# Layer 0's stores of two steps sent in one run, ahead of the keys' transfers of the same step

## The chip, the cores and the metric

The kernel runs on one NeuronCore of a Trainium2 chip. The time is that of the device for one execution, in microseconds (us). Before the change three runs took 5833.54, 5835.1 and 5843.29 us; their median is 5835.1. The engines are TensorE (PE in the profile, PEld for its weight loads), VectorE (DVE), ScalarE (ACT), GpSimd (POOL) and SyncE (SP). SP computes nothing here: it issues the DMA transfers, one after the other in the order of the program.

## The reference, cut to what matters

A picture of 4 x 16 x 512 x 512 fp32 values goes through four layers. The change is in layer 0, a block with windowed attention; the three others are stacks of convolutions and are only named here.

```python
def _L0_conv_ref(x, ...):                       # C = 16, HEADS = 2, WS = 8, HID = 64
    pos = conv_general_dilated(x, pos_w, 3x3, feature_group_count=Cc)
    x = x + pos + pos_b
    xt = transpose(x.reshape(B, Cc, H * W), (0, 2, 1))
    y = _aff(xt, alpha1, beta1, color1)         # y @ color.T * alpha + beta
    win = y cut into windows of 8 x 8           # 4 * 64 * 64 windows of 64 tokens
    q, k, v = win @ qkv_w.T + qkv_b             # q scaled by hd ** -0.5
    attn = softmax(einsum('bhnd,bhmd->bhnm', q, k))
    out = einsum('bhnm,bhmd->bhnd', attn, v) @ proj_w.T + proj_b
    x = xt + out put back in place
    h1 = gelu(_aff(x, alpha2, beta2, color2) @ fc1_w.T + fc1_b)
    return x + (h1 @ fc2_w.T + fc2_b)

x = _L0_conv_ref(x, ...)
x = _L1_conv_ref(x, ...)    # quantised 3x3 convolution, batch norm over the picture, clip
x = _L2_conv_ref(x, ...)    # two 3x3 convolutions with a residual
x = _L3_conv_ref(x, ...)    # 3x3 convolution, then a pointwise layer of 128
```

Layer 1 quantises by the largest absolute value of its whole input. So layer 0 has to end before layer 1 can round its first value. The kernel therefore keeps the maximum of each piece of layer 0's result in a tile `peak`.

## The kernel before, in words

**Steps.** `window_attention` is layer 0. It cuts the picture into 64 steps. A step works on 64 columns of all strips, which gives 128 partitions of four row groups (`U` = `V` = 4) and 8 windows each. Each step has two halves. The first is the attention: a loop over k from 1 to 7 with a piece before it and one behind it, so eight pieces in all. Piece k turns eight key tiles (`values`, a transpose on TensorE, L338), multiplies keys by queries (`scores`, L353), takes the exponential on ScalarE (L361), multiplies by the values (`attend`, L374), and divides (`divide`: two transposes L389 and a reciprocal L394 on VectorE, a multiplication L396 on GpSimd). The second half is the projection, the two layers of the MLP (L421 with Gelu at L426), and, mixed with them, the depthwise convolution (L287) and the queries (L319) of the steps that follow. ScalarE loads its table for the exponential at the end of a step (L574) and the one for Gelu between the halves (L540). So the time from a load at L574 to the next at L540 is that of the first half, and from L540 to L574 that of the second.

**The order.** Layer 0 runs in an order written out by hand (`manual_schedule`) for all five queues: each engine takes its instructions as the Python code emits them. A DMA waits on SP until what it reads is written and what it overwrites is read. SP's later transfers stay behind it.

**The keys.** `y2` holds the keys of all windows of a step in the form that `scores` and `values` need. There is one such buffer, in four quarters. When a quarter has been read by pieces 2q and 2q + 1 of step n, `turn_keys` (L310) fills it with the keys of step n + 1: 8 transfers of 32 KB, 32 in a step. They are called behind the division at k = 1, 3, 5 and 7.

**The outputs.** `output` (fc2 on TensorE, L432, and the sum with the residual on VectorE, L437) is called at the head of the step behind its own, between the first scores and the loop over k. It writes `xo`, one buffer that takes the results of two steps, an even one and the odd one behind it. When the odd step's part is there, `store` puts 32 stores of 64 KB into a Python list, with 8 largest values to be taken. The results of the steps n - 2 and n - 1 are therefore complete at the head of step n, where n is even. `send` takes stores from the list and issues them at L90 on SP; each writes 16 partitions of `xo` to the picture `x1` in the chip's memory. The next `output`, at the head of the odd step n + 1, writes `xo` again; it has to wait until the stores have read it.

**Banks.** `output` uses the four PSUM banks 5, 4, 6 and 7. `values(1)`, at k = 1, writes bank 6 and has to wait until the sum at L437 has read it.

**The load.** At the end of a step SP issues the load of the picture's part for the step four ahead (L185, 1320 KB into one of two buffers `x`). It waits until the depthwise convolution has read the buffer. The data are used two steps later.

The lines around the change are these:

Of the kernel before, what the change touches and what calls it, by code (L numbers as in the profile page):

```python
# [86 lines left out]
def _store_block(nc, x1, src, b, r0, cols, queues=None):  # L87

    rows = x1.rearrange("m (r c) b x -> (m r) c b x", r=2)[r0 + 1 : r0 + 1 + WS, :, b, cols]
    (next(queues) if queues else nc.sync).dma_start(rows.rearrange("m c x -> c m x"), src)  # L90
# [53 lines left out]
def window_attention(ctx: ExitStack, tc, xw, x1, hots, m, v, peak):  # L144
# [15 lines left out]
    U = V = 4  # L160
# [122 lines left out]
    def depthwise(n, tap, u):  # L283

        dy, dx = divmod(tap, 3)
        for vv in range(V):
            nc.tensor.matmul(  # L287
                bank(u)[quad(vv)], taps[quad(u), tap, :],
                xts[n][quad(u), vv, dy : dy + WS, dx : dx + BW],
                start=tap == 0, stop=tap == 8,  # L290
            )

    def position(n):

        y = px.tile([P, U, N], F32, tag="y", name=f"y{n}", bufs=3)
        for u in range(U):
            if u // 2:
                nc.scalar.activation(  # L298
                    by_window(y[:, u]), by_row(bank(u)), AF.Identity, bias=v("pos_b")
                )  # L300
            else:
                nc.vector.tensor_scalar(  # L302
                    by_window(y[:, u]), by_row(bank(u)), v("pos_b"), None, ALU.add
                )
        return y

    def turn_keys(y, vv):
        for u in range(U):
            for w in range(2):
                nc.sync.dma_start(  # L310
                    y2[32 * u + C * w : 32 * u + C * w + C, vv, :, w, :],
                    y[32 * vv + C * w : 32 * vv + C * w + C, u, :].rearrange(
                        "p (j t) -> p j t", t=T
                    ),
                )

    def query(y, h, vv, b, scalar=False):
        for u in range(U):
            nc.tensor.matmul(  # L319
                b[quad(u)], wg[h][quad(vv)], y[quad(vv), u, :], start=True, stop=True  # L320
            )
        out, src = g[:, vv, :, h, :], b.rearrange("p (j t) -> p j t", t=T)
        if scalar:
            nc.scalar.activation(out, src, AF.Identity, bias=gb[:, h : h + 1])
        else:
            nc.vector.tensor_scalar(out, src, gb[:, h : h + 1], None, ALU.add)
# [6 lines left out]
    def values(k):  # L333

        vv, jl = k // 2, 4 * (k % 2)
        b, t = bank(4 + 2 * (k % 2)), yts[k % 3]
        for jj in range(4):
            nc.tensor.transpose(  # L338
                b[:, P * jj : P * jj + P],
                y2[:, vv, jl + jj].rearrange("p w t -> p (w t)"), m("ident"),  # L340
            )
        src = b.rearrange("p (a w c) -> p a w c", w=2, c=C)
        if 0 < k < 7:
            nc.scalar.copy(t[:, :, 0:3:2], src)
        else:
            nc.vector.tensor_copy(t[:, :, 0:3:2], src)  # L346

    def scores(k, n):

        vv, jl = k // 2, 4 * (k % 2)  # L350
        for i, jj in ((0, 0), (0, 1), (1, 0), (0, 2), (1, 1), (0, 3), (1, 2), (1, 3)):
            for u in (2 * i, 2 * i + 1):
                nc.tensor.matmul(  # L353
                    bank(u)[:, P * jj : P * jj + P],
                    y2[quad(u), vv, jl + jj].rearrange("p w t -> p (w t)"),
                    g[quad(u), vv, jl + jj].rearrange("p h t -> p (h t)"),
                    start=True, stop=True,
                )
        e = px.tile([P, U, 4, P], F32, tag="e", name=f"e{n}_{k}", bufs=3)
        for i in range(2):  # L360
            nc.scalar.activation(  # L361
                e[:, 2 * i : 2 * i + 2].rearrange("p u j t -> p u (j t)"),
                pairs[i], AF.Exp,
            )
        return e

    def attend(e, k):

        t = yts[k % 3]
        for jj in range(4):  # L370
            for u in range(U):
                for w in range(2):
                    half = slice(64 * w, 64 * w + 64)
                    nc.tensor.matmul(  # L374
                        bank(4 + 2 * (k % 2) + w)[quad(u), P * jj : P * jj + P],
                        t[half, U * jj + u, w : w + 2].rearrange("p d c -> p (d c)"),
                        e[half, u, jj, :],
                        start=True, stop=True,
                    )

    def part(t, k):
        vv, jl = k // 2, 4 * (k % 2)
        return t[:, vv, jl : jl + 4].rearrange("p j h t -> p (j h t)")
# [18 lines left out]
    def turn_back(t, k):  # L402
        nc.vector.transpose(part(o, k), t.rearrange("p b w c -> p (b w c)"))
# [25 lines left out]
    def output(y, xo, hids, us, banks, n):  # L429

        for k, (vv, hd) in enumerate(hids):
            nc.tensor.matmul(  # L432
                bank(banks[k // 4])[quad(vv)], m("fc2"), hd, start=True, stop=True
            )
        at = BW * (n % 2)
        for u, i in zip(us, banks):
            nc.vector.tensor_tensor(  # L437
                xo[:, u, :, at : at + BW].rearrange("p a (j x) -> p a j x", x=WS),
                by_window(bank(i)), by_window(y[:, u]), ALU.add,
            )  # L440
        if n % 2:
            store(xo, n // 2, us)
# [22 lines left out]
    def send(k, queues=None):  # L465
        for _ in range(min(k, len(stores))):
            src, u, r, cb = stores.pop(0)
            _store_block(nc, x1, src, u, r, slice(XW * cb, XW * cb + XW), queues)
# [40 lines left out]
    for n in range(STEPS):  # L509
        more, ahead = n + 1 < STEPS, n + 2 < STEPS  # L510
        taken, asked = [0] * U, [0] * V

        def block(what, i, b, scalar=False):
            at = i % 4
            if what == "q" and more:
                query(ys[n + 1], asked[at], at, b, scalar)
                asked[at] += 1
            elif what == "d" and ahead:
                depthwise(n + 2, taken[at], at)
                taken[at] += 1  # L520
                if taken == [9] * U:
                    ys[n + 2] = position(n + 2)

        values(0)
        es, ts = {0: scores(0, n)}, {}
        if last:

            output(*last)
        for k in range(1, 8):
            es[k] = scores(k, n)  # L530
            values(k)
            attend(es[k - 1], k - 1)
            ts[k - 1] = divide(k - 1, n, nc.gpsimd)
            if 1 < k < 7:
                turn_back(ts[k - 2], k - 2)
            if k % 2 and more:
                turn_keys(ys[n + 1], k // 2)
            highest_output()
            send(5)
        nc.scalar.preload_act_table_set("gelu_and_others")  # L540
        attend(es[7], 7)
        ts[7] = divide(7, n, nc.gpsimd)
        for k in (5, 6, 7):
            turn_back(ts[k], k)
        free = iter((4, 5, 6, 7, 4, 5))
        for i, what in enumerate("qqddddqqqqdddddd"):
            block(what, i, bank(next(free)) if what == "q" else None, True)
        if more:
            highest(n + 1)
        highest_output()  # L550
        y = ys.pop(n)
        project(y)
        if n % 2 == 0:
            xo = px.tile([P, U, WS, XW], F32, tag="xo", name=f"xo{n}", bufs=1)
        if not more:
            flag = bounded()

        hids, units = [], itertools.cycle((6, 7, 4, 5))  # L560
        for i, what in enumerate("ddddhdhddhqhddhqhddhdhddhdhddhdhddhdhddddhdh"):
            if what == "h":
                q = len(hids)
                hids.append(hidden(y, q // 4, i % 4, bank(next(units)), n))
                if not more and q in (5, 9, 13):
                    u = q // 4 - 1
                    output(y, xo, hids[q - 5 : q - 1], (u,), (u,), n)
                    send(8, queues)
            else:
                block(what, i, bank(next(units)) if what == "q" else None)  # L570
        if n + 4 < STEPS:
            xts[n + 4] = load(n + 4)
        if more:
            nc.scalar.preload_act_table_set("natural_log_exp_and_others")  # L574
        last = (y, xo, hids, range(U), (5, 4, 6, 7), n)
# [795 lines left out]
```

## Time and profile before

| | |
|---|---|
| median of three runs | 5835.1 us |
| profiled execution | 5832.97 us |
| its span | 5831.2 us |
| mean granted TensorE clock | 0.987 |
| TensorE busy | 5512.4 us |
| ScalarE busy | 3464.1 us |
| VectorE busy | 3723.4 us |

The span is the time from the first to the last instruction that the profile records; the time of the execution is 1.8 us longer. Layer 0 reaches to about 3250 us of the span; layers 1 to 3 follow. The page's second part cuts the span into 40 slices of 145.8 us. Its digits are busy shares in tenths; layer 0 has slices 1 to 22.

The transfers of layer 0, from the page's sixth part, are:

```
x<-in_xw_dram SPq DMA_DIRECT2D x64, 1320.0 KB
y<-y SPq DMA_DIRECT2D x2048, 32.0 KB
x<-xo SPq DMA_DIRECT2D x1008, 64.0 KB
```

The first are the loads, the second the keys, the third the stores; 16 more stores of the last step go through GpSimd's queue. From 169 to 3190 us of the span, a store keeps SP for 303 ns at least, 435 in the median and 2017 at most; a key transfer for 585, 598 and 2139 ns. This is the time of the issue, not of the transfer.

In a line of the timeline the numbers are the start in us from the span's start, the time taken in us, the engine (SPq is SP's DMA queue), the line of the kernel, the operation, what is written and read, and how many instructions were merged. In brackets stands how long the engine was idle before and what ended this.

### The profile page before, as it was taken

To read this page: it belongs to the slowest core of one execution; us is meant where nothing else is said; L and a number is where in the kernel's file an instruction comes from. 1 tells how busy PE (TensorE), PEld (TensorE's weight loads), DVE (VectorE), ACT (ScalarE), POOL (GpSimd) and SP (SyncE) were. 2 spreads that over 40 slices of the span, in tenths; PEclk is the share of its full clock that TensorE was granted. 3 is DMA by queue.
4 is the path that set the end of the run, shared out by engine and by line. 5 is a ranking of instruction groups with operands and counts; after the bars stand their busy time and mean duration, and the time that the engine had idled before them with its cause. 6 is when DMAs were issued, how large, how long until landed. Compare 5 with 4: busy or idle time off the path is not lost. (4 is left out here: it accounts for less than half of the span.)

```text
span 5831.2 us, 268523 instructions
## 1 busy us (share of the span) xinstructions
PE 5512.4 (95%) x120912; PEld 3058.4 (52%) x120912; DVE 3723.4 (64%) x5806; ACT 3464.1 (59%) x4739; POOL 707.4 (12%) x692
## 2 busy tenths in 40 slices
PE   7999999999999999999999676999999999999999
PEld 5666666666666666666666333333333333333333
DVE  4666666666666666666666564666666666666666
ACT  4777777777777777777776453444444444444444
POOL 1111111111111111111111451000000000000000
PEclk9999999999999999999999898999999999999999
DMA  2232323233333333332332796666666666666663
GB/s 78 69 77 68 81 67 72 69 79 70 78 72 75 75 72 77 71 79 69 79 70 47 170 252 169 168 169 171 165 171 167 169 171 166 170 167 170 171 165 103
DMA packets 626194, 677.47 MB, mean 116 GB/s; under 512 B 355856, under 2 KB 485008, under 8 KB 616848
## 3 DMA queue, kind: packets, MB, share of 16 engines
q1 hardware_dynamic: 624240, 658.76, 47.3%
q8 instruction: 953, 15.61, 1.1%
q14 instruction: 201, 1.65, 0.1%
q0 software_dynamic: 512, 1.05, 0.1%
q10 hardware_dynamic: 288, 0.39, 0.0%
HBM read 222.45 MB, written 134.48 MB: 61 GB/s over the span
## 5 line engine op out<-in xcount | busy, mean ns | idle before, releaser
L361 ACT ACTIVATE e<-pair 128x1024 f32<-128x1024 f32 x1024 | 992.9, 1022 | 436.7 <-PE pair L353 436.0
L287 PE MATMUL pair<-x,taps 32*32 32x512 f32 x18432 | 1082.2, 600 | 2.2 <-DVE y L302 1.2
L1205 ACT ACTIVATE hid<-tb,vec 128x512 f32<-128x512 f32 x1024 | 620.0, 688 | 518.1 <-PE tb L1197 518.0
L389 DVE STREAM_TRANSPOSE a<-bank 128x512 f32<-128x512 f32 x1024 | 669.8, 692 | 346.5 <-PE bank L374 313.3
L396 POOL TENSOR_TENSOR t<-a,r 128x512 f32<-128x512 f32 x512 | 542.0, 1059 | 2662.2 <-DVE r L394 2598.5
L426 ACT ACTIVATE hid<-bank,f1b 128x512 f32<-128x512 f32 x1024 | 648.3, 687 | 345.2 <-PE bank L421 281.6
L353 PE MATMUL pair<-g,y 32*128 32x128 f32 x16384 | 762.8, 288 | 29.5 <-ACT y L298 25.8
L353 PEld LDWEIGHTS pair<-g,y 32*128 32x128 f32 x16384 | 650.4, 187 | 189.6 <-issue 77.4
L421 PE MATMUL bank<-y,fc_e 32*32 32x512 f32 x8192 | 738.3, 606 | 1.0 <-DVE y L414 1.0
L1207 DVE TENSOR_SCALAR hid<-tb,vec 128x512 f32<-128x512 f32 x1024 | 695.7, 742 | 2.7 <-PE tb L1197 2.6
L1197 PE MATMUL tb<-ye,mat 32*128 32x512 f32 x4096 | 637.7, 624 | 0.3 <-DVE hid L1207 0.3
L374 PE MATMUL bank<-e,yt 64*32 64x128 f32 x32768 | 610.0, 276 | 28.3 <-DVE yt L346 21.4
L287 PEld LDWEIGHTS pair<-x,taps 32*32 32x32 f32 x18432 | 495.4, 103 | 171.2 <-issue 66.3
L374 PEld LDWEIGHTS bank<-e,yt 64*32 64x32 f32 x32768 | 465.6, 106 | 127.3 <-issue 99.1
L1217 PE MATMUL tb<-hid,mat 128*32 128x512 f32 x4096 | 466.0, 595 | 41.6 <-DVE hid L1207 41.6
L1197 PEld LDWEIGHTS tb<-ye,mat 32*128 32x128 f32 x4096 | 267.0, 183 | 323.4 <-issue 219.9
L1122 PE MATMUL tb<-zo,cw 64*32 64x512 f32 x3096 | 362.8, 594 | 14.8 <-issue 8.9
L338 PE MATMUL bank<-mat,y 128*128 128x128 f32 x2048 | 338.9, 288 | 36.1 <-DVE xo L437 36.0
L1122 PE MATMUL tb<-xo,cw 64*32 64x512 f32 x3096 | 365.0, 599 | 8.4 <-issue 6.6
L1122 PE MATMUL tb<-xe,cw 64*32 64x512 f32 x3072 | 360.3, 599 | 0.0
L1122 PE MATMUL tb<-ho,cw 64*32 64x512 f32 x3072 | 355.2, 591 | 3.1 <-issue 3.1
L1122 PE MATMUL tb<-ze,cw 64*32 64x512 f32 x3072 | 356.8, 594 | 0.0
(180 smaller groups left out, 7051.7 us busy)
## 6 DMA issues: line engine op xcount, KB each, us to landing
x<-in_xw_dram SPq DMA_DIRECT2D x64, 1320.0 KB
zo<-ze SPq DMA_DIRECT2D x512, 128.5 KB
ho<-he SPq DMA_DIRECT2D x512, 128.5 KB
xo<-xe SPq DMA_DIRECT2D x512, 128.5 KB
y<-y SPq DMA_DIRECT2D x2048, 32.0 KB
tx<-x SPq DMA_DIRECT2D x256, 256.0 KB
out_dram<-xe SPq DMA_DIRECT2D x128, 512.0 KB
x<-xo SPq DMA_DIRECT2D x1008, 64.0 KB
```

The source lines that it names most:

```text
L287: nc.tensor.matmul(bank(u)[quad(vv)], taps[quad(u), tap, :], xts[n][quad(u), vv, dy : dy + WS, dx : dx + BW], start=tap == 0, stop=tap == 8,)
L353: nc.tensor.matmul(bank(u)[:, P * jj : P * jj + P], y2[quad(u), vv, jl + jj].rearrange("p w t -> p (w t)"), g[quad(u), vv, jl + jj].rearra ...
L361: nc.scalar.activation(e[:, 2 * i : 2 * i + 2].rearrange("p u j t -> p u (j t)"), pairs[i], AF.Exp,)
L374: nc.tensor.matmul(bank(4 + 2 * (k % 2) + w)[quad(u), P * jj : P * jj + P], t[half, U * jj + u, w : w + 2].rearrange("p d c -> p (d c)"), ...
L389: nc.vector.transpose(a[:, 512 * w : 512 * w + 512], bank(4 + 2 * (k % 2) + w))
L396: engine.tensor_tensor(t.rearrange("p b w c -> p w b c"), top, r.unsqueeze(3).to_broadcast([P, 2, 16, C]), ALU.mult,)
L421: nc.tensor.matmul(b[quad(k)], fc1[quad(vv), quad(k)], y[quad(vv), u, :], start=True, stop=True,)
L426: nc.scalar.activation(hd, b, AF.Gelu, bias=f1b)
L1122: nc.tensor.matmul(p[r][_quad(2 * f + w)], weights[_half(r), odd, dx, :], src[_half(r), f, dx : dx + W], start=dx == 0, stop=dx == 2,)
L1197: nc.tensor.matmul(p[q], w1[_quad(q), 1 - par, :], inner(src)[_quad(q), f, :], start=True, stop=True,)
L1205: nc.scalar.activation(hd, p[q], AF.Relu, bias=v("l3_b1"))
L1207: nc.vector.tensor_scalar(hd, p[q], v("l3_b1"), 0.0, ALU.add, ALU.max)
```

## The change

At k = 1, behind the first division and ahead of the first `turn_keys`, `send(8 * U)` issues up to 32 stores. The `send(5)` at the end of each of the seven passes is gone. `store` fills the list for each even step alone, so the call finds 32 stores in the even steps 2 to 62 and none in the odd ones. The stores of the last two steps are sent by other calls, which stay as they are.

```diff
             ts[k - 1] = divide(k - 1, n, nc.gpsimd)
             if 1 < k < 7:
                 turn_back(ts[k - 2], k - 2)
+            if k == 1:
+                send(8 * U)
             if k % 2 and more:
                 turn_keys(ys[n + 1], k // 2)
             highest_output()
-            send(5)
         nc.scalar.preload_act_table_set("gelu_and_others")
         attend(es[7], 7)
```

## The prediction

> **What bounds the kernel now.** I read the page first (shares, the 40 slices), then the waits of the first stage by total, then two neighbouring steps in the timeline, then the DMA share microsecond by microsecond.
>
> ```profile
> PE 5512.4 (95%) x120912; PEld 3058.4 (52%) x120912; DVE 3723.4 (64%) x5806; ACT 3464.1 (59%) x4739; POOL 707.4 (12%) x692
> ...
> PE   7999999999999999999999676999999999999999
> ...
> DMA  2232323233333333332332796666666666666663
> ```
>
> TensorE is the bound from slice 2 to the end, and the change touches only layer 0, slices 1 to 22. There the 16 DMA engines are busy 20 to 30% of the time: a mean that hides bursts. What counts is each piece of idle time on PE. The waits of 200 to 3100 us, PE's own first, then DVE's on xo and the two largest of SP's queue (these three for 200 to 3000):
>
> ```profile
> PE bank L338 <- DVE xo L437: 36.0, 24, 3.1
> PE pair L353 <- ACT y L298: 24.5, 59, 0.4
> PE bank L374 <- DVE yt L346: 19.4, 32, 0.8
> ...
> DVE xo L437 <- DMA x<-xo: 103.2, 19, 7.1
> ...
> SPq L185 <- PE bank L421: 404.7, 28, 15.5
> SPq L310 <- PE bank L338: 360.8, 71, 7.9
> ```
>
> The columns are total us, times, longest. PE's largest wait is 36.0 us in 24 pieces, for xo, and xo waits in turn for the stores of the xo before it. All 24 pieces are in odd steps. Step 19 (odd, its outputs at 1022 us) beside step 18 (even, at 970 us), DVE, then PE, then SP:
>
> ```profile
> 967.53 0.69 DVE L346 COPY yt<-bank 128x512 f32<-128x512 f32 x1
> 970.87 1.50 DVE L437 TENSOR_TENSOR xo<-bank,y 128x512 f32<-128x512 f32 x2 [2.65 <-PE bank L432]
> ...
> 1016.75 0.69 DVE L346 COPY yt<-bank 128x512 f32<-128x512 f32 x1
> 1022.93 2.48 DVE L437 TENSOR_TENSOR xo<-bank,y 128x512 f32<-128x512 f32 x4 [5.49 <-PE bank L432]
> ...
> 974.46 0.66 PE L338 MATMUL bank<-mat,y 128*128 128x128 f32 x4
> ...
> 1024.87 0.66 PE L338 MATMUL bank<-mat,y 128*128 128x128 f32 x4 [1.15 <-DVE xo L437]
> ...
> 1012.43 5.72 SPq L310 DMA_DIRECT2D y<-y  x8
> 1018.20 2.11 SPq L90 DMA_DIRECT2D x<-xo  x2
> 1020.41 0.38 SPq L185 DMA_DIRECT2D x<-in_xw_dram  x1
> ```
>
> In the even step the first output comes 970.87 - 967.53 = 3.34 us after the values' copy; in the odd one 1022.93 - 1016.75 = 6.18 us. The page names PE as the releaser, but the L432 matmuls begin equally early in both steps (969.68 and 1018.88, 2.15 and 2.13 us after the copy); what came last is the store whose issue ended at 1020.31, 2.6 us before. PE then stands 1.15 us before L338, since values(1) needs the bank that the output has yet to read. So a store that lands late in an even step holds up the output of the odd step behind it.
>
> **What the skill says.** (1) The Trainium skill, "DMA: Bandwidth & Descriptors", section "Anatomy of one DMA": the DMA engines wait for no semaphore; a wait is made on the issuing sequencer, before dispatch, so everything behind it in that queue waits too. The trace agrees: SP stands 404.7 us before L185 and 360.8 us before L310. (2) The same section puts the fixed cost of a transfer at about 2.0 us, mostly the receipt of the last write; here 2.6 us lie between the end of the last store's issue and the instruction it releases. (3) "TensorE: Matmul & The Clock Gate", section "Part 1: The HAM clock gate": after an idle window of about 3.4 us the clock drops to half. Here much shorter waits were followed by it at times: the granted clock was 0.50 in 228 to 231, 328 to 331, 628 to 630, 826 to 828, 2014 to 2016 and 2703 to 2705 us, each just after a wait for xo of 1.75 to 3.11 us; after two waits of 2.65 and 2.75 us it stayed 1.00.
>
> **The change, part by part.** Nothing is computed differently. PE, DVE, ACT and POOL keep their instructions and order; on SP, in each even step from 2 to 62, 32 stores go ahead of 32 keys' transfers, in place of 8 keys, 10 stores, 8, 10, 8, 10, 8, 2. Nothing goes to POOL's queue. In odd steps, send finds nothing, before and after.
>
> *SP's time in an even step.* Bursts of ten stores in steps 16 and 18 took 6.19, 7.31, 5.73, 5.82, 6.23 and 5.64 us, mean 6.15, so 32 take 19.7 us. Runs of eight keys took 6.11, 7.23, 5.96, 6.40, 5.77, 6.95 and 5.72, mean 6.31, so 32 take 25.2 us. The sum, 44.9 us, is what SP did before too (975.14 to 1020.31 without a gap).
>
> *The new wait.* The first store waits for the first output of xo, about 971.6 in step 18, earlier than the scores for which SP waited until 975.14. The stores are issued by 971.6 + 19.7 = 991.3 and land by 993.9. The output of step 19 can use xo from about 1020.1 (1016.75 + 3.34): the cover is 26 us, where now it is -2.8.
>
> *What is queued behind.* The keys run from 991.3 to 1016.5. Quarter 0 has landed by 991.3 + 6.3 + 2.6 = 1000.2 and is first read by L338 at 1015.99: 16 us of cover. The last quarter lands at 1019.1 and is read by values(6), the sixth of a series with some 3 us between members from 1023 on, so after 1038: 19 us. By then PE has long passed the scores that free y2, so the keys wait for nothing. The load of the next x (L185) waits for PE until about 1015 anyway; it goes at 1016.5 instead of 1020.41, and its data are read a whole step later. So its burst no longer stands where xo is wanted. All this costs nothing.
>
> *What the odd steps gain.* PE's waits alone are 36.0 us. A second way includes what hangs on them (slow clock, ScalarE's late start): the time from one table load of ScalarE (L574, start of the scores) to the next (L540). Over the 30 odd steps 3 to 61 it is 27.10 us in the mean, over the 30 even ones 4 to 62 it is 25.78. The six odd steps without a PE wait (29, 43, 45, 49, 51, 55) have 25.67 to 26.09, mean 25.83, so what is late next costs nearly nothing. Gain: 30 x (27.10 - 25.83) = 38 us. The second way holds the slow windows too (six of 3.4 us at half clock, some 10 us lost); that it isn't larger shows that PE makes good part of what it waited. The other half of a step (L540 to L574) is 23.5 us in even steps and 22.1 to 23.2 in odd ones, whatever the first half was; I leave it. Step 63 has no gain to take: the clock was at half there in 3187 to 3204 us.
>
> *Sum.* The profiled execution took 5833.0 (span 5831.2 and 1.8 around it); less 38 is 5795. The median of the runs is 2.1 above the profiled one: 5835.1 - 38 = **5797**.
>
> *Bounds.* The one thing that the trace doesn't show is 32 stores in a row. From below: the median issue is 0.435 us and 0.05 between, 15.4 us in all. From above: at the stores' pace the engines are 75 and 79% busy (983 to 985 us), so a queue could form; I take 0.62 us each as in the bursts of ten. The cover of the keys ends only where a store takes (1015.99 - 971.6 - 8.9) / 32 = 1.11 us. The gain lies between 28 us (the slow windows turn up elsewhere) and 50 (the odd steps fall to the floor of 25.62, 44 us, and the second half gives a little): 5785 to 5807.
>
> **The rivals.**
> - *Given back.* The odd step gets through its first half sooner and stands somewhere else as long: the waits for ScalarE at L353 or for the fc1 matmuls grow. For it: the second half of odd steps varies by 1.1 us for no visible cause. Against it: steps 51 and 49, without a wait, had 25.62 and 25.94 and then 22.06 and 22.89, no longer than after a wait. Time 5824 to 5840, say 5832.
> - *The keys come late: slower.* If 32 stores without a pause crowd the DMA engines so that each takes 1.25 us, twice the burst's, the stores end at 971.6 + 40 = 1011.6, quarter 0 lands at 1020.5 and PE waits 4.5 us at the head of every odd step: 31 x 4.5 - 38 = +102, 5937 us. It decides from 1.11 us a store on. For it: the 75 to 79%. Against it: in bursts of ten issue goes on at 0.43 us to the end, apart from single slow ones.
> - *It doesn't do what it says.* xo would still wait, since its write asks for the last transfer of every semaphore lane. Against it: the lanes' last stores are those of the same xo, and they now end 26 us earlier. 5835 us.
>
> **How the numbers follow.** The gain as worked out 0.80, given back 0.11, keys late 0.07, without effect 0.02. A measurement of this kernel can tell about 0.2%, 11.7 us, from no change. The first case lies beyond that nearly whole and a little of the second does: faster 0.81, same 0.12, slower 0.07. The first case's own range, 5785 to 5807, is widened to 5781 to 5823, which leaves out the deepest gains, most of the given-back case and all of the slower one, 2 in 10 together.
>
> **What would show it.** Right: no wait of PE for xo at L338 in odd steps, and none of DVE for the DMA x<-xo; L437 some 3.3 us after the values' copy in odd steps too; one run of 32 stores of 16 to 20 us on SP in an even step, then 32 keys without a wait; mean L574 to L540 near 25.8 in all steps; fewer half-speed windows in layer 0. Wrong: PE waiting for a DMA y<-y at L338 or L353; stores of over 1 us each; second halves of odd steps above 23 us; the same 36 us under another name.

## The result and the profile after

The changed kernel took 5782.85 us in the median of four runs (5772.67 to 5786.44), the kernel before, run beside it, 5834.32 (5831.92 to 5843.29). The ratio is 0.9906, with a 95% interval from 0.9889 to 0.9923: 0.94% faster. Applied to the 5835.1 us from which the prediction started this is 5780 us, 55 us less, where 38 were forecast. The medians alone differ by 51.5. The profiled execution took 5786.44 us, 46.5 less than the one before (5832.97), and its span is shorter by as much.

The page of the changed kernel, first and second part, and from the third the row that the experiments lead to:

```profile
PE 5500.3 (95%) x120912; PEld 3057.2 (53%) x120912; DVE 3731.7 (65%) x5806; ACT 3462.5 (60%) x4739; POOL 707.4 (12%) x692
...
PEclk9999999999999999999999998999999999999999
DMA  2333333333323232323331896666666666666663
...
q8 instruction: 953, 15.61, 1.2%
```

The shares of the engines show next to nothing of the gain. PE's waits from 200 to 3100 us do:

```profile
PE pair L353 <- ACT y L298: 24.6, 60, 0.4
PE bank L374 <- DVE yt L346: 21.4, 42, 1.1
PE bank L374 <- issue: 5.5, 14, 0.6
```

The columns are total us, times, longest. The row for xo at L338, 36.0 us in 24 pieces before, is gone; the two that stood below it changed by 2 us at most. "Issue" means that PE waited for nothing that the profile shows; what it was is worked out below. Step 19 again, now at 997 us, with the even step ahead of it: VectorE, TensorE, then SP's queue.

```profile
997.33 0.69 DVE L346 COPY yt<-bank 128x512 f32<-128x512 f32 x1
1000.67 1.50 DVE L437 TENSOR_TENSOR xo<-bank,y 128x512 f32<-128x512 f32 x2 [2.65 <-PE bank L432]
...
1004.25 0.66 PE L338 MATMUL bank<-mat,y 128*128 128x128 f32 x4
...
951.93 19.89 SPq L90 DMA_DIRECT2D x<-xo  x32
971.91 26.56 SPq L310 DMA_DIRECT2D y<-y  x32
998.57 0.53 SPq L185 DMA_DIRECT2D x<-in_xw_dram  x1
```

The first output comes 3.34 us after the values' copy, as in an even step, and PE reaches L338 without a wait. The 32 stores take one piece of 19.89 us on SP. The last is issued by 971.82 us; with the 2.6 us from issue to release that the kernel before showed, xo is free 26 us before it is written again at 1000.67.

Where did the time go? I cut the span by ScalarE's table loads. Layer 0 here means the stretch from the load at the start of step 1 to the one in the middle of step 63. It fell from 3097.0 to 3055.0 us. The first halves of the 30 odd steps from 3 to 61 lost 41.8 us (27.10 to 25.70 in the mean), their second halves some 2, and the even steps gained 3. The rest of the span fell from 2613.4 to 2608.6, which lies within the spread that the runs below show for it.

### The profile page after: what moved, and what is told of

Same layout as the page of the kernel before. It is cut to its first block, busy times and chain, and to the rows that moved or that the text cites. A ratio compares the mean times of both kernels' runs of the same rounds, so it can differ in the third digit from the quotient of the medians.

```text
span 5784.7 us, 268523 instructions
## 1 busy us (share of the span) xinstructions
PE 5500.3 (95%) x120912; PEld 3057.2 (53%) x120912; DVE 3731.7 (65%) x5806; ACT 3462.5 (60%) x4739; POOL 707.4 (12%) x692
## 3 DMA queue, kind: packets, MB, share of 16 engines
q8 instruction: 953, 15.61, 1.2%
q14 instruction: 201, 1.65, 0.1%
## 5 line engine op out<-in xcount | busy, mean ns | idle before, releaser
L1123 PE MATMUL tb<-he,cw 64*32 64x512 f32 x3072 | 355.4, 589 | 0.0
```

The source lines that it names most:

```text
L1123: nc.tensor.matmul(p[r][_quad(2 * f + w)], weights[_half(r), odd, dx, :], src[_half(r), f, dx : dx + W], start=dx == 0, stop=dx == 2,)
```

## The experiments

The runs form three groups: e, f with g, and h. Each group ran on one chip, beside the kernel before, but the groups ran on different chips, on which the kernel before took 5840.7, 5858.8 and 5873.8 us in the median. Medians can be compared inside a group only; ratios go further, but the intervals of most neighbours overlap. Each trace is of one run: for the changed kernel, e4, f2, g1, g2, h1 and h4 the slowest of their runs, for e3 and f1 the fastest. The last two columns are totals of PE's waits for issue from 200 to 3100 us, over all halves of all steps and in the first halves of odd steps alone.

| run | median us | ratio, 95% interval | layer 0 us | odd first half, mean us | PE waits for issue, us | of these in odd first halves |
|---|---|---|---|---|---|---|
| before (trace) | | | 3097.0 | 27.10 | 6.3 | 0.0 |
| changed kernel | 5782.85 | 0.9906 (0.9889 to 0.9923) | 3055.0 | 25.70 | 7.3 | 0.3 |
| e1_send6 | 5801.16 | 0.9929 (0.9909 to 0.9949) | 3070.5 | 26.25 | 19.8 | 10.4 |
| e2_behind_keys | 5798.30 | 0.9918 (0.9897 to 0.9939) | 3072.5 | 26.05 | 19.2 | 6.9 |
| e3_last | 5821.19 | 0.9968 (0.9952 to 0.9983) | 3078.2 | 26.72 | 4.8 | 1.1 |
| e4_after_again | 5787.75 | 0.9906 (0.9884 to 0.9927) | 3057.7 | 25.72 | 6.9 | 1.1 |
| f1_load_first | 5790.66 | 0.9884 (0.9866 to 0.9902) | 3059.6 | 25.77 | 13.9 | 0.7 |
| f2_load_late | 5870.74 | 1.0016 (1.0006 to 1.0025) | 3154.3 | 28.51 | 63.1 | 53.9 |
| g1_peak_moved | 5796.29 | 0.9870 (0.9847 to 0.9894) | 3063.7 | 25.79 | 16.4 | 2.0 |
| g2_both | 5785.23 | 0.9868 (0.9849 to 0.9886) | 3062.7 | 25.80 | 16.8 | 2.2 |
| h1_after_third | 5804.62 | 0.9879 (0.9852 to 0.9906) | 3071.8 | 25.86 | 19.0 | 3.3 |
| h2_both_again | 5782.15 | 0.9848 (0.9821 to 0.9876) | 3055.8 | 25.77 | 15.4 | 1.6 |
| h3_late_in_four | 5819.98 | 0.9913 (0.9890 to 0.9937) | 3092.3 | 26.06 | 27.2 | 7.0 |
| h4_all_in_four | 5813.13 | 0.9906 (0.9881 to 0.9930) | 3105.1 | 26.24 | 32.2 | 10.8 |

### Is it the wait for xo? (e1 to e4, one chip)

e1, on the kernel before:

```diff
-            send(5)
+            send(6)
```

> The kernel before with send(6) for send(5): the last two stores of an even step go ahead of its last eight keys' transfers instead of behind them; everything else stays. The wait theory (all that counts is that the last store lands before the next step's output wants xo, some 3.3 us after the values' copy): the last store lands some 6.3 us earlier, cover about +3.5 us where it was -2.8, so most odd steps lose their wait; PE waits for xo at L338 under 6 us in all, first half of odd steps 25.7 to 26.0 us in the mean, 30 to 45 us less than before, close to the changed kernel (ratio 0.990 to 0.995). The rival (what helps is that keys and the next load are moved, or that stores stand in one run): stores are still spread and the load still goes at the end of the same queue, so 0 to 15 us less than before (ratio 0.997 to 1.000).

PE's wait for xo is gone altogether (no such row), with stores spread and keys in front: the wait theory holds. The ratio, 0.9929, is within the range foreseen. But layer 0 is only 26.5 us shorter than before, and odd first halves are 26.25 us, above the 25.7 to 26.0 foreseen. Other waits have grown:

```profile
PE bank L374 <- issue: 10.1, 23, 0.7
PE pair L353 <- issue: 6.2, 7, 2.0
```

In odd first halves PE waited 10.4 us for issue here and not at all in the kernel before, with the load of the next x issued equally late (2.29 and 2.32 us after the table load in the mean).

e2, on the changed kernel:

```diff
-            if k == 1:
-                send(8 * U)
             if k % 2 and more:
                 turn_keys(ys[n + 1], k // 2)
+            if k == 1:
+                send(8 * U)
```

> The changed kernel with send(8 * U) behind the first turn_keys instead of ahead of it. The wait theory: stores are issued from about 981.5 + 0 to + 20 us on the scale of the kernel before, cover about 16 us instead of 26, both ample: same time as the changed kernel within 0.2%, layer 0 within 5 us. The rival (going ahead of the keys is what counts): half or more of the 51 us comes back.

No wait for xo either, and odd first halves of 26.05 us. The median is 10.6 us above e4 (the intervals overlap), a fifth of the 51 us; in the traces layer 0 is 14.8 us longer than in e4. That is less than the rival's half and more than the 5 us of the wait theory. Neither had it right. What e1 and e2 have more of than the changed kernel stands in e2's waits:

```profile
PE bank L374 <- issue: 13.6, 29, 1.3
PE pair L287 <- issue: 2.5, 5, 0.9
PE pair L353 <- issue: 2.0, 6, 0.7
```

These are waits for issue again. Step 55 of e2, whose table load is at 2772.74 us: SP, the DMA share (columns: stretch, us, PE busy, clock, DMA share, GB/s), PE.

```profile
2775.77 0.53 SPq L185 DMA_DIRECT2D x<-in_xw_dram  x1
...
2778.00:2779.00 1.00, 1.00 (x35) 1.00 0.90 380
2779.00:2780.00 1.00, 1.00 (x60) 1.00 1.10 465
2780.00:2781.00 1.00, 1.00 (x31) 1.00 0.79 297
...
2781.86 0.65 PE L374 MATMUL bank<-e,yt 64*32 64x128 f32 x27
2783.80 0.85 PE L374 MATMUL bank<-e,yt 64*32 64x128 f32 x37 [1.30 <-issue]
```

The load of the next x goes 3.0 us after the table load and fills the DMA engines until 2781. In the trace's DMA records, queue q8 (953 packets, 15.61 MB on the page, each of 16 KB) brings instructions. In an odd first half one starts about every 4 us; here one came at -2.8 us from the table load and the next not before 8.8 us, after the burst, and PE ran dry in the middle of a group of 64. In the mean of odd steps the load was issued 2.3 us after the table load in e1 and e2, and 1.35 us before it in e4: SP starts 3.5 us sooner there, as stores need no scores. I call this the fetch theory: the burst keeps PE's instructions waiting.

That a wait for issue is a wait for instructions can be read from the traces. In all fourteen together PE has 522 such waits over 0.15 us between 200 and 3100 us, and each of them ended 1.0 to 1.7 us after the end of a q8 packet. Of moments taken at random in f2 or h1, only 15 or 16 in 100 lie so. A late load doesn't always cost: in e2, 10 of the 29 odd first halves with a load have such a wait, and others with as late a load take 25.6 us.

e3, on the changed kernel, with the same two lines behind the keys and `k == 7` for `k == 1`.

> send(8 * U) at k = 7 behind the last turn_keys: one run of 32 stores, but last in the queue. The wait theory: SP ends at the same time as in the kernel before (about 45 us of work from the first key on), so xo waits as long or longer: odd first halves 27.0 us or more in the mean, time within 0.3% of before or slower (ratio 0.998 to 1.010). The rival (one run instead of pieces, or less traffic mixed with keys, is what helps): 20 us or more faster than before.

```profile
PE bank L338 <- DVE xo L437: 27.0, 24, 3.5
```

PE still waits for xo in 24 pieces, and odd first halves are 26.72 us, near the 27.10 before: stores in one run give little by themselves. The time was 0.32% under before all the same; this and the 26.72 lie outside what I had foreseen. The last store is issued 0.26 us sooner after the table load than in the kernel before (1.39 against 1.65 in the mean), and nine us of wait and half of the six slow clock windows went with it; whether that is all was not tried.

e4, the changed kernel:

> The changed kernel unchanged, for a second trace and the spread. Layer 0 from the start of step 1 to the middle of step 63: 3055 us in the first trace. Theory A: the 51.5 us between the medians are 42 us of layer 0 plus chance outside it, so layer 0 comes out at 3055 within 4 us again and the rest of the span differs by some us either way. Theory B: layers 1 to 3 became faster too, so the rest of the span (from the table load in the middle of step 63 on) is 2608.6 within 1.5 us again, 4.7 us less than in the trace before.

Layer 0 came out at 3057.7, the rest at 2611.6: theory A. Over all traces the rest lies between 2601.9 and 2617.6 us, without visible relation to what was changed. How far layer 0 of the kernel before differs from run to run is not known, since that kernel was traced once.

### Is it the load? (f1, f2; g1, g2)

f1, on e2:

```diff
-            if k % 2 and more:
+            if k % 2 and more and (k < 7 or n % 2):
                 turn_keys(ys[n + 1], k // 2)
...
             xts[n + 4] = load(n + 4)
+        if more and n % 2 == 0:
+            turn_keys(ys[n + 1], 3)
```

> e2_behind_keys with one thing moved: in even steps the last quarter of the keys goes behind the load of the next x, so that SP reaches the load before TensorE frees the buffer and issues it about 2.35 us before the table load of the odd step, as in even steps, where e2 issues it 2.25 us after. The fetch theory (e2 lies 15 us behind the changed kernel because the load's burst of some 4 us holds up TensorE's instruction fetches of 16 KB, queue 8, in the dense first half of odd steps): TensorE's waits for issue fall from 19.2 us to 5 to 10, odd first halves from 26.05 to 25.6 to 25.8 us, layer 0 to within 4 us of the changed kernel's 3055 to 3058. The rival (e2 lies behind because its keys and stores stand in that order, or by chance): no change from e2, 26.0 us and 3072.

The load went 2.24 us ahead of the table load in the mean, odd first halves fell to 25.77 and layer 0 to 3059.6, near the changed kernel. The waits for issue fell less than foreseen, from 19.2 to 13.9; but in odd first halves, where the burst had stood, they fell from 6.9 to 0.7. Stores and first keys stand in e2's order still, which speaks against that order as the cause. This is another chip than e2's, and f1's trace is the fastest of its runs; e2 was not run beside it.

f2, on the changed kernel:

```diff
+            if k == 1 and n % 2 and n + 3 < STEPS:
+                xts[n + 3] = load(n + 3)
...
-        if n + 4 < STEPS:
+        if n % 2 and n + 4 < STEPS:
             xts[n + 4] = load(n + 4)
```

> The changed kernel with the load that stood at the end of each even step issued in the next, odd step behind its first eight keys, about 11 us after the table load instead of 1 us before it. xo's stores land as early as in the changed kernel. The fetch theory: the burst falls at 12 to 17 us, in the middle of the dense half, fetches due then come up to 4 us late, TensorE's waits for issue rise from 7 to over 20 us and odd first halves from 25.7 to over 26.2 us: 15 to 40 us slower than the changed kernel. The theory that xo's wait is all: same as the changed kernel within 5 us, since no data are late.

No data were late and xo never waited, yet the whole gain was gone: 80 us above f1 on the same chip, far over what the fetch theory had asked for.

```profile
PE bank L374 <- issue: 40.4, 38, 2.9
PE pair L353 <- ACT y L298: 23.7, 58, 0.4
PE bank L374 <- DVE yt L346: 18.9, 36, 0.8
PE pair L353 <- issue: 17.3, 13, 3.6
```

Step 23 of f2 (table load at 1231.34): the load's issue, the DMA share, PE.

```profile
1244.00 0.59 SPq L185 DMA_DIRECT2D x<-in_xw_dram  x1
...
1247.00:1248.00 1.00, 1.00 (x68) 1.00 1.10 454
1248.00:1249.00 1.00, 1.00 (x32) 1.00 0.88 359
...
1249.07 0.33 PE L338 MATMUL bank<-mat,y 128*128 128x128 f32 x1
1252.11 0.80 PE L338 MATMUL bank<-mat,y 128*128 128x128 f32 x3 [2.71 <-issue]
```

Fetches were at 6.0, 10.7 and 18.4 us of this step, none from 13.9 to 18.0, while the load's packets ran; the half took 30.9 us. In step 21 one came at 13.1, just ahead of the burst, and the half took 26.1. So it is in all 29 odd steps whose load was moved: no fetch began in the first 3.1 us of the burst, and the next began near its end. This is the clearest showing of the fetch theory. What its forecast left out is the clock: in 200 to 3100 us f2 has 15 half-speed stretches, 61.4 us in all, where f1 has none. By an estimate from this, half of it or some 31 us was lost there, beside 49 us more of waits for issue; the traces of f2 and f1 differ by 95 us in layer 0.

g1, on the changed kernel, is a try at the even steps:

```diff
-        highest_output()
         y = ys.pop(n)
...
+            if i == 20:
+                highest_output()
```

> The changed kernel with the eighth largest value of xo (L452, 0.67 us on VectorE) of each even step taken in the middle of the MLP half, where VectorE is idle, instead of right ahead of the projection's sums (L414). If those sums hold up even steps (second half 23.5 us against 22.5 in odd ones), the second half of even steps falls by 0.5 to 1.0 us and the kernel is 15 to 30 us faster than the changed one. If TensorE's own work sets the even half: no change.

The second half of even steps is 23.34 us in the mean, where the changed kernel has 23.52 on another chip: a third of what was expected at least. One reduction ahead of L414 isn't what makes even steps a microsecond longer than odd ones. g2 puts f1's edit on top:

> g1_peak_moved and in addition the last quarter of an even step's keys behind the load, as in f1. The fetch theory: the load goes always at -2.35 us, up to 5 us less than g1 (the changed kernel's loads go at -2.4 to +1.2 already). Otherwise: same as g1.

With all loads at -2.35 us, where g1 has -0.93 in the mean of odd steps, it came out as g1 (0.9868 beside 0.9870).

### On one chip, and in pieces (h1 to h4)

> The changed kernel once more, beside the three below on the same chip, as their measure. Ratio to before 0.989 to 0.992; layer 0 within 5 us of 3055; TensorE's waits for issue from 200 to 3100 us 6 to 9 us (16 us if the higher figure of the last runs belongs to the chip and not to the kernels).

On this chip the changed kernel itself waits 19.0 us for issue and layer 0 takes 3071.8, outside the 5 us; the ratio, 0.9879, is just better than foreseen, since the kernel before lost more. Its odd loads go at -1.08 us, much as in e4 (-1.35). Only 3.3 of the 19.0 us lie in odd first halves (1.1 of 6.9 in e4). So what waits for issue cost outside the stretch that the load decides differed between these chips, and the load's part is best read inside a group, or in odd first halves alone.

> g2_both once more beside the changed kernel: the last quarter of an even step's keys behind the load, the eighth largest value in the MLP half. If its ratio of 0.9868 was a gain and not another chip: 8 to 25 us below h1. If it was the chip: within 8 us of h1.

22 us below h1 (0.9848 beside 0.9879; the intervals overlap). The traces agree, 16 us less in layer 0. But h2 has two edits, and about 9 of the 16 us are in the second halves of even steps (23.46 to 23.15 us), where the largest value was moved; odd first halves, the load's place, gave less than 3. So this pair doesn't show a gain by the load. Of the versions tried this has the lowest ratio, 1.5% under the kernel before.

h3 is f2 with its load cut into four, issued behind the keys of k = 1, 3, 5, 7 in odd steps; h4 does this with all loads from step 1 on.

```diff
+    def load_part(k, vv):
+        if not vv:
+            xts[k] = xin.tile([P, V, WS + 2, BW + 2], F32, tag="x", name=f"x{k}")
+        nc.sync.dma_start(xts[k][:, vv], xw[k][:, vv])
...
+            if k % 2 and n % 2 and n + 3 < STEPS:
+                load_part(n + 3, k // 2)
```

> f2_load_late with the late load cut into four transfers of 330 KB, one behind each eight keys of the odd step; the same bytes at the same stage, as late or later. The fetch theory (it is the unbroken burst of 4 us that keeps a 16 KB fetch waiting): each piece keeps a fetch for about 1 us, which the instructions already fetched cover; TensorE's waits for issue fall from 63 us to under 20, odd first halves from 28.5 to under 26.2 us, time within 15 us of h1. The rival (the load's bytes in the first half cost by sharing memory or DMA engines with keys, or SP's queue gets too full): odd first halves over 27 us.

The same bytes as late as in f2, but waits for issue of 27.2 us instead of 63.1 (7.0 instead of 53.9 in odd first halves), one half-speed stretch of the clock instead of 15, and odd first halves of 26.06 instead of 28.51 us: the unbroken burst was most of it. The chip is another one, but the changed kernel's own traces differ by 12 us of waits and 0.14 us between e4 and h1, far less than this. In step 23 a fetch now came at 15.5 us, between two pieces. It is not all: 27.2 is over the 20 foreseen, and the kernel is 15 us above h1.

> The changed kernel with every load from step 1 on, even and odd, cut into four and issued behind the keys of the next step, none at the head of a step. In even steps the stores go ahead, the keys and pieces follow. The fetch theory: no burst over 1 us is left in layer 0, TensorE's waits for issue are the lowest of all (under 6 us), time 0 to 10 us below h1. The rival: SP has about 1.5 us more to issue and pieces stand between keys, 0 to 20 us above h1.

Here the fetch theory missed. With no long burst left in these steps the waits for issue were 32.2 us, not under 6, and the time 8.5 us above h1 (the intervals overlap). All 64 of these waits, too, ended 1.2 to 1.6 us after a fetch, so fetches still came late, without a burst of 4 us. Which traffic held them up, and by how much, stays open. A load at the head of a step did better than one cut up; there PE starts few instructions (matmuls and weight loads, in the changed kernel 14 to 34 a microsecond from 4 us ahead of the table load to 4 us behind it, and 37 to 91 in the 20 us that follow).

## Why the mechanism was right, and where the size was wrong

- *SP's time, the cover, the keys.* As worked out: 19.89 us for the stores of the step shown (19.7), 26.56 for its keys (25.2), no wait of PE for keys, 26 us of cover for xo.
- *The wait for xo.* Gone in all odd steps, as foreseen, and with it the slow clock: in 200 to 3100 us no half-speed window is left in the changed kernel, where the one before had six. The Trainium skill ("TensorE: Matmul & The Clock Gate", "Part 1: The HAM clock gate") speaks of idle windows of about 3.4 us; the waits that came ahead of the slow windows here were shorter, and the windows went when the waits went.
- *The step that failed: the sum and its bounds.* The forecast gain was 38 us, the measured one 55. Layer 0 gave 42 of them, within the 28 to 50 that the bounds allowed, and 4 above the 38. The other 13 lie in what the sum put at nothing: it set a gain read from one execution, and from layer 0 alone, against the median of three runs that differed by 10 us, and its bounds held nothing for the rest of the span or for the spread of the runs. The range was then widened downwards by 4 us alone, to 5781; measured were 5780. The rest of the span gave 4.7 us in this pair. The two profiled executions, 46.5 us apart, lay 2.1 below the median of 5835.1 and 3.6 above that of the changed kernel; the ratio gives 2.6 more than those medians. Over 18 runs on the chip of e1 to e4 the kernel before spread from 5807.8 to 5861.8. e4 had a ratio of 0.9906 again, so the 55 us may not be chance; what is in them beyond the 42 stays open, since no edit was tied to it and the kernel before was traced once.
- *What the odd steps gain* is mis-sized by the 4 us, 41.8 measured for 38, and the load is the likely reason. The prediction priced the earlier load at nothing ("All this costs nothing"). By the traces of e2 the wait alone is worth 30 x (27.10 - 26.05) = 31 us, and the changed kernel's 30 x (26.05 - 25.70) = 10 us more go with the load, which it issues 3.4 us sooner. This split is an estimate from single traces on different chips. Most of the 10 us were in the forecast unseen: the six odd steps without a wait, its measure of what is late next, are those in which the load went earliest (0.71 to 1.46 us after the table load, in all others 1.74 or later), which fits their 25.83 us beside the 26.05 of e2, whose loads went 2.25 us after it in the mean. The page of the kernel before couldn't show this: with the wait for xo, PE had no wait for issue in odd first halves, and without it, in e1, 10.4 us.
- *Readings.* The lowest of the six steps is 25.62 us, not 25.67. One of the six slow windows is 6.8 us long, so they make 23.9 us. The long slow stretch near the end of layer 0 runs from 3177 to 3194 us, not from 3187 to 3204. 32 issues of 0.435 us with 0.05 between make 15.5 us. None of this enters the 38 us. The 2.0 us of the Trainium skill ("Anatomy of one DMA") are given there for transfers that GpSimd issues; SP issues the stores here, and the sums use the 2.6 us of the trace.
- *The rivals.* Given back: no, the second halves of odd steps are 22.5 us, 22.6 before. Keys late: no. Without effect: no.

## What to carry to other kernels

When a wait is taken away, ask what else the idle engine was getting for free: here a load's burst hid behind it that then held up instruction fetches. Issue the stores of a single buffer ahead of work that has slack, and try a large load where the engine that bounds the kernel starts few instructions. When a gain is read from one trace, put the spread between runs into its bounds.

## What was not expected of the hardware

In f2 a load of 1320 KB kept the DMA engines at 0.8 to 1.1 of their time for about 4 us. In all 29 odd steps no instruction fetch (16 KB, most of them 0.9 to 1.5 us long) began in the first 3.1 us of it, and TensorE then stood up to 3.6 us for issue. In f2, sixteen half-speed stretches of the clock, of 3.4 or 6.8 us, fell between 142 and 2971 us, where the changed kernel had none. The waits for issue differed by chip: the same kernel had 6.9 us on one and 19.0 on another, most of it outside the odd first halves.
